# A Macaron layer with a selective scan on one core: the softplus correction in the other half of delta's tile, two buffers for normalised tiles, sixteen weight blocks

## The chip, the cores and the metric

The kernel runs on one core of a Trainium2 chip. The metric is device time in microseconds (us) from launch to end, the median of several runs. A core has a matrix engine (TensorE, PE, with a separate path for weight loads, PEld), a vector engine (DVE), a scalar engine (ACT), GpSimd (POOL) and SyncE (SP), whose queue issues nearly all transfers of this kernel. Each engine works through its own queue in order, and they meet at semaphores.

## The reference

The input is x of shape (4, 1024, 512): four sequences of 1024 tokens, 512 wide, all in float32. Three residual blocks follow each other:

```python
x = x + 0.5 * ffn(layernorm(x))       # gated FFN, 512 -> 1408 -> 512
x = x + mamba(layernorm(x))           # selective scan, inner width 1024, 16 states
x = x + 0.5 * ffn(layernorm(x))       # the same FFN weights again
# ffn:   g = (x @ gate_w.T) * gate_s; u = (x @ up_w.T) * up_s
#        out = ((silu(g) * u) @ down_w.T) * down_s
# mamba: h, gate = split(x @ W_in.T); h = silu(causal_conv4(h) + conv_b)
#        ts, Bm, Cm = split(h @ Wx.T), each rms-normalised
#        delta = softplus(ts @ Wdt.T + dt_bias)
#        s = exp(delta * A) * s + delta * Bm * h      # over time, per channel and state
#        y = (sum over states of s * Cm) + D * h; out = (y * silu(gate)) @ Wout.T
```

## The kernel before

The tokens are cut into 16 chunks (`NCS`) of 256 tokens (`T`), four to a sequence. Chunk k is one stage of the main loop. In stage k the scan of chunk k runs beside "background" work: the gate products of chunk k, the projection back (`tail`) of chunk k - 1, the input projection, convolution and parameters of chunk k + 1, and an FFN over three or four tiles of 128 tokens. `BESIDE[k]` says how many of these tiles belong to the first FFN and how many to the second. An opening (`front`) does the FFN of the first four tiles, and an ending (`back_end`) that of the last four.

The scan of a stage is 32 units: eight channel blocks `i` times four state groups `g`. A unit takes exponentials on ACT (L573), forms delta * u * B on POOL (L578, tile `sb`), scans on DVE (L582), multiplies by C on DVE (L592), and a later fold sums over states on PE (L604, tile `yps`). Before that, delta and delta * u of a channel block must lie on the scan's partition layout: `rows` writes a tile `dd` to DRAM and `spread` reads it back four times as `rep`.

`head(k, i)` makes `dd` for two channel blocks at a time, in eight small steps called chores, one of which is done in each unit. With t = dt + bias, softplus is computed as max(t, 0) + log(1 + exp(-|t|)). ACT writes |t| to `z` and max(t, 0) to `de`, the first half of `dd` (L498, L499), then exp and log (L502, L503). POOL makes the rounding error of 1 + z: e = (1 + z) - 1 (L521), e - z (L506), and takes it from the log (L507). Then POOL completes `de` (L510) and writes delta * u into the second half of `dd` (L511). `dd` has two buffers; `z`, `e` and `lg` have one each.

Normalisation: `stats` takes mean and variance on DVE, POOL makes the factors (`roots`, L214 to L216), and ACT writes the normalised tile `xn` (L218). `flip` transposes it with four PE instructions (L235), and ACT copies the result out (L238). The steps are deferred by one background piece each; `flips` begins tile n + 2 when it has flipped tile n. `xn` comes from a pool with three buffers.

Weights: blocks of 128 x 512 floats stream from DRAM for every chunk through a ring of `RING` = 14 tiles, with the tag `w`. `queue` lists all pieces of work that use blocks, in the order in which they are emitted. After each piece, `do` gives its blocks back and calls `fetch`, which emits loads, in that order, until `LEAD` = 12 blocks are held:

```python
while queue and sum(map(len, held.values())) < LEAD:
    ...
    t = ring.tile([P, H], F32, tag="w", name=f"w_{name}")
```

A piece of `gate`, `up` or W_in holds one block until it is emitted. The eleven blocks of `down_w` and the eight of `Wout` are held until the last part of their stage of work; the projection back is emitted in four parts (two token tiles, each in two halves). When a block of `down_w` comes in for the first time, in the opening, DVE scales it (L133) and it is stored back to DRAM. All loads, stores, rows and spreads are issued by SP in the order in which they are emitted (`load`, L101). Stores of x1 and x2 are emitted two pieces after their sum (`write(2)`).

Of the kernel before, what the change touches and what calls it, by code (L numbers as in the profile page):

```python
# [8 lines left out]
F32 = mybir.dt.float32  # L9
# [4 lines left out]
P = 128  # L14
B, L, H = 4, 1024, 512
# [7 lines left out]
T = 256  # L23
# [8 lines left out]
HEAD = 11  # L32
BEHIND = 1
HALVES = 14
LEAD = 12
FRONT = 5
RING = 14

BESIDE = [(3, 0), (3, 0), (2, 2), (2, 2), (1, 2), (2, 2), (2, 2), (2, 1), (2, 2), (2, 2), (2, 1), (2, 2), (2, 2), (1, 2), (0, 3), (0, 3)]

# [2 lines left out]
def macaron_kernel(ctx: ExitStack, tc: tile.TileContext, a: dict, out: bass.AP):  # L43
# [2 lines left out]
    small = ctx.enter_context(tc.tile_pool(name="small", bufs=4))  # L46
    p1 = ctx.enter_context(tc.tile_pool(name="p1", bufs=1))
    p2 = ctx.enter_context(tc.tile_pool(name="p2", bufs=2))
    p3 = ctx.enter_context(tc.tile_pool(name="p3", bufs=3))
    p4 = ctx.enter_context(tc.tile_pool(name="p4", bufs=4))  # L50
    px = ctx.enter_context(tc.tile_pool(name="px", bufs=HALVES))
    p8 = ctx.enter_context(tc.tile_pool(name="p8", bufs=8))
    ring = ctx.enter_context(tc.tile_pool(name="ring", bufs=RING))
    dram = ctx.enter_context(tc.tile_pool(name="scratch", bufs=1, space=bass.MemoryType.DRAM))
# [65 lines left out]
    def fetch():  # L120

        while queue and sum(map(len, held.values())) < LEAD:
            w = queue[0]
# [30 lines left out]
    def defer(parts, emit):  # L154

        deferred.append([parts, emit])
# [45 lines left out]
    def stats(src, name):  # L202

        stt = small.tile([P, nc.vector.BN_STATS_DIM], F32, tag="st", name=f"st{name}")
        mv = small.tile([P, nc.vector.BN_AGGR_DIM], F32, tag="mv", name=f"mv{name}")
        ve = small.tile([P, 1], F32, tag="ve", name=f"ve{name}")
        rs = small.tile([P, 1], F32, tag="rs", name=f"rs{name}")
        nb = small.tile([P, 1], F32, tag="nb", name=f"nb{name}")
        nc.vector.bn_stats(stt, src)
        nc.vector.bn_aggr(mv, stt)  # L210
        xn = p3.tile([P, H], F32, tag="xn", name=f"xn{name}")

        def roots():
            pin(nc.gpsimd.tensor_scalar(ve, mv[:, 1:2], EPS, None, ALU.add))  # L214
            pin(nc.gpsimd.tensor_tensor(rs, ve, neg_half[:, 0:1], ALU.pow))
            pin(nc.gpsimd.tensor_scalar(nb, mv[:, 0:1], rs, -1.0, ALU.mult, ALU.mult))  # L216

        left = [roots, lambda: pin(nc.scalar.activation(xn, src, AF.Identity, bias=nb, scale=rs))]  # L218

        def more():  # L220
            if left:
                left.pop(0)()
                defer(1, more)

        defer(1, more)
        return xn, left
# [16 lines left out]
    class FFN:  # L243
# [17 lines left out]
        def stats(self, t):  # L261
            return stats(self.x[t], f"f{self.name}_{t}")
# [84 lines left out]
    def prep_stats(k, j):  # L347
        return stats(st[k]["xi", j], f"m{k}_{j}")
# [128 lines left out]
    def head(k, i):  # L477

        d = st[k]
        nm = f"{k}_{i}"  # L480
        dp = ps_m.tile([P, 2, T], F32, tag="mm", name=f"dp{nm}")
        z = p1.tile([P, 2, T], F32, tag="z", name=f"z{nm}")
        e = p1.tile([P, 2, T], F32, tag="e", name=f"e{nm}")
        lg = p1.tile([P, 2, T], F32, tag="lg", name=f"lg{nm}")
        dd = p2.tile([P, 2, 2, T], F32, tag="dd", name=f"dd{nm}")
        de = dd[:, :, 0, :]

        def products():
            for q in range(2):
                nc.tensor.matmul(  # L490
                    dp[:, q, :], lhsT=w_dt[:, (i + q) * P : (i + q + 1) * P], rhs=d["tsT"],
                    start=True, stop=True,
                )

        def split():
            for q in range(2):
                b = dt_b[:, i + q : i + q + 1]
                pin(nc.scalar.activation(z[:, q, :], dp[:, q, :], AF.Abs, bias=b))  # L498
                pin(nc.scalar.activation(dd[:, q, 0, :], dp[:, q, :], AF.Relu, bias=b))  # L499

        def logs():
            pin(nc.scalar.activation(z, z, AF.Exp, scale=-1.0))  # L502
            pin(nc.scalar.activation(lg, z, AF.Ln, bias=1.0))  # L503

        def correct():
            pin(nc.gpsimd.tensor_tensor(e, e, z, ALU.subtract))  # L506
            pin(nc.gpsimd.tensor_tensor(lg, lg, e, ALU.subtract))  # L507

        def complete():
            pin(nc.gpsimd.tensor_tensor(de, de, lg, ALU.add))  # L510
            pin(nc.gpsimd.tensor_tensor(dd[:, :, 1, :], de, d["u"][:, i : i + 2, :], ALU.mult))  # L511
            d["dd", i] = dd[:, 0]
            d["dd", i + 1] = dd[:, 1]

        return [
            products,
            split,
            logs,
            lambda: None,
            lambda: None,  # L520
            lambda: pin(nc.gpsimd.tensor_scalar(e, z, 1.0, 1.0, ALU.add, ALU.subtract)),  # L521
            correct,
            complete,
        ]
# [251 lines left out]
    settle()  # L776
    between = gate_0[FRONT:]
    chores = head(0, 0)
    while chores:
        chores.pop(0)()  # L780
# [3 lines left out]
    for w in between[:2]:  # L784
        do(w)
    chores = head(0, 2)
    while chores:
        chores.pop(0)()
# [6 lines left out]
    for k in range(NCS):  # L795
# [18 lines left out]
        for i in range(NI):  # L814
            for g in range(NS):
                unit(k, i, g)
                if i == 0 and k:
                    gated(k - 1, NI - NS + g)
                if len(summed) >= NS + BEHIND:
                    for _ in range(NS):  # L820
                        add_up()
                n += 1
                done, vector = done + unit_t, vector + unit_v
                while parts and (
                    done * total_v < vector * total
                    or (length - len(parts)) * (units - HEAD) < upto * min(n, units - HEAD)
                ):
                    c, v = step()
                    done, vector = done + c, vector + v
                k2, i2 = ahead(2)  # L830
                if i % 2 == 0 and g == 2 and k2 < NCS:
                    assert not chores
                    rows(k2, i2)
                    rows(k2, i2 + 1)
                k2, i2 = ahead(3)
                if i % 2 == 1 and g == 1 and k2 < NCS:
                    while more and i2 == 0 and ready[k] in parts:
                        c, v = step()
                        done, vector = done + c, vector + v
                    chores += head(k2, i2)  # L840
                    chores.pop(0)()
# [77 lines left out]
```

## Time and profile before

| what | value |
|---|---|
| median of 3 runs | 3204.71 us (3203.93 to 3205.31) |
| the profiled execution: its own time / its span | 3208.17 us / 3206.3 us |
| granted TensorE clock, mean over the span | 0.986 |
| transfers | 506.43 MB, mean 158 GB/s |
| weight loads W_in, gate_w, up_w (256 KB each), median from issue to landing | 3.6, 4.0, 4.1 us |
| L578 POOL scan product, 128x512 | 1275 ns, 1024 times |
| L582 DVE scan with a state, 128x256 | 740 ns, 1536 times |
| L218 ACT normalised tile of the FFN, 128x512 | 814 ns, 56 times |

The span runs from the first to the last instruction; the execution's own time has what lies around it as well. "Busy" is the time in which an engine had an instruction of the program in work. A row of waits reads: who waited, for whom, us in total, how often, the longest. For SP, whose instructions are all the sequencer's, a wait is counted from its instruction before. A row of a group reads: line, engine, operation, out<-in, shapes, count, then busy us and mean ns of one, then the engine's idle time before it and who ended that. "L521" is line 521 of the kernel's file. PE matmul counts are of the chip's instructions, two for each float32 matmul of the program.

### The profile page before, as it was taken

The page shows a single profiled execution, that of the slowest core. Times are in us where ns is not written, and L with a number is a line of the kernel's source. Part 1 is how long each engine was busy: PE and PEld are TensorE (multiplying, and loading weights), DVE is VectorE, ACT ScalarE, POOL GpSimd, SP SyncE. Part 2 cuts the span into 40 slices and gives each one's busy share as a digit, 9 for nine tenths or more (in the row PEclk, how much of TensorE's full clock was granted, in tenths as well). Part 3 has the DMA queues.
Part 4 walks back from the last instruction along what each step waited for, and adds up shares of the span by engine and source line. Part 5 has one row for each costly group of instructions (what it writes and reads, how often), then busy time and mean ns, then how long its engine had stood idle before and what let it go on. Part 6 is the DMA issues. An engine that isn't in the chain of part 4 may idle for free.

```text
span 3206.3 us, 41927 instructions
## 1 busy us (share of the span) xinstructions
PE 3059.7 (95%) x12448; PEld 1644.7 (51%) x12448; DVE 2477.8 (77%) x4981; ACT 1780.1 (56%) x3531; POOL 1938.5 (60%) x1895
## 2 busy tenths in 40 slices
PE   8988899999999999999999999999999999899999
PEld 3554454545555454545545454554555455454434
DVE  1259788888869887887988788798878779798931
ACT  3265555747465664646565474656557475656530
POOL 0066758566766766666675756667575667658610
PEclk9999999999999999999999999999999999999999
DMA  5364566556566655645665654656565564566531
GB/s 171 113 174 119 158 188 171 161 137 184 134 174 181 178 161 148 184 123 160 191 178 159 164 164 123 183 165 171 168 178 161 140 186 132 170 183 178 169 94 43
DMA packets 287427, 506.43 MB, mean 158 GB/s; under 512 B 32097, under 2 KB 50273, under 8 KB 287201
## 3 DMA queue, kind: packets, MB, share of 16 engines
q1 hardware_dynamic: 285616, 503.31, 55.8%
q8 instruction: 100, 1.64, 0.2%
q14 instruction: 127, 1.03, 0.1%
q10 hardware_dynamic: 1584, 0.45, 0.1%
HBM read 442.03 MB, written 61.60 MB: 157 GB/s over the span
## 4 chain that ended last, share of the span: by engine, by line
PE 63%; DVE 21%; ACT 6%; POOL 5%; issue 5%; DMA 1%; DVEq 0%; SPq 0%; POOLq 0%; ACTq 0%
DVE da L582 12%; PE fo L319 12%; PE gate_w L273 12%; PE up_w L273 9%; PE hp L376 5%; PE op L637 5%; PE gp L545 5%; PE yps L604 5%; DVE sb L592 4%; POOL sb L578 3%; ACT da L573 2%; PE gate_wp L273 1%; PE gate_we L273 1%; PE dp L490 1%; PE foe L319 1%
## 5 line engine op out<-in xcount | busy, mean ns | idle before, releaser
L578 POOL TENSOR_TENSOR sb<-rep,bc 128x512 f32<-128x512 f32 x1024 | 1279.4, 1275 | 421.3 <-PE yps L604 302.8
L582 DVE TENSOR_TENSOR_SCAN da<-da,state,sb 128x256 f32<-128x256 f32 x1536 | 1059.7, 740 | 250.9 <-ACT da L573 215.6
L573 ACT ACTIVATE da<-rep,a_w 128x256 f32<-128x256 f32 x2048 | 899.5, 472 | 508.9 <-DVE sb L592 488.0
L592 DVE TENSOR_TENSOR sb<-da,bc 128x512 f32<-128x512 f32 x1024 | 688.8, 680 | 1.7 <-issue 0.4
L273 PE MATMUL gate_w<-fxT,w_gate_w 128*128 128x384 f32 (+1 forms) x1408 | 564.2, 547 | 8.6 <-ACT hd L287 6.3
L273 PE MATMUL up_w<-fxT,w_up_w 128*128 128x384 f32 (+1 forms) x1408 | 557.8, 546 | 3.0 <-DVE hd L304 2.4
L319 PE MATMUL fo<-w_down_w,hd 128*128 128x512 f32 x1232 | 549.4, 599 | 0.0
L273 PEld LDWEIGHTS gate_w<-fxT,w_gate_w 128*128 128x128 f32 x1408 | 268.1, 193 | 256.2 <-issue 154.9
L604 PE MATMUL yps<-sb,fold 128*32 128x256 f32 x4096 | 332.0, 389 | 62.8 <-DVE sb L592 54.1
L273 PEld LDWEIGHTS up_w<-fxT,w_up_w 128*128 128x128 f32 x1408 | 260.7, 190 | 254.1 <-issue 150.8
L582 DVE TENSOR_TENSOR_SCAN da<-da,sb 128x256 f32<-128x256 f32 x512 | 322.6, 679 | 78.6 <-ACT da L573 62.2
L319 PEld LDWEIGHTS fo<-w_down_w,hd 128*128 128x128 f32 x1232 | 230.1, 192 | 273.0 <-issue 271.5
L521 POOL TENSOR_SCALAR e<-z 128x512 f32<-128x512 f32 x64 | 124.4, 1944 | 237.3 <-ACT z L502 223.1
L604 PEld LDWEIGHTS yps<-sb,fold 128*32 128x32 f32 x4096 | 127.7, 110 | 271.4 <-DVE sb L592 122.9
L376 PE MATMUL hp<-mxT,w_W_in 128*128 128x259 f32 x1024 | 244.3, 386 | 23.1 <-issue 12.4
L545 PE MATMUL gp<-mxT,w_W_in 128*128 128x256 f32 x1024 | 244.7, 388 | 4.0 <-ACT dd L499 3.3
L376 PEld LDWEIGHTS hp<-mxT,w_W_in 128*128 128x128 f32 x1024 | 192.5, 191 | 83.5 <-issue 30.4
L637 PE MATMUL op<-w_Wout,u 128*128 128x512 f32 x512 | 228.1, 595 | 0.3 <-POOL u L616 0.3
L545 PEld LDWEIGHTS gp<-mxT,w_W_in 128*128 128x128 f32 x1024 | 195.4, 193 | 63.0 <-issue 19.8
L387 DVE SCALAR_TENSOR_TENSOR u<-hp,conv_w,u 128x256 f32<-128x256 f32 x384 | 178.0, 473 | 14.7 <-ACT u L380 12.2
L287 ACT ACTIVATE hd<-gate_w,gate_s 128x384 f32<-128x384 f32 (+1 forms) x176 | 110.5, 629 | 130.4 <-PE gate_w L273 129.6
L304 DVE SCALAR_TENSOR_TENSOR hd<-up_w,up_s,hd 128x384 f32<-128x384 f32 (+1 forms) x176 | 118.2, 672 | 69.0 <-PE up_w L273 68.9
(112 smaller groups left out, 2649.9 us busy)
## 6 DMA issues: line engine op xcount, KB each, us to landing
rep<-row SPq DMA_DIRECT2D x512, 256.0 KB, 4.9
w_W_in<-in_W_in_dram SPq DMA_DIRECT2D x256, 256.0 KB, 3.6
w_gate_w<-in_gate_w_dram SPq DMA_DIRECT2D x198, 256.0 KB, 4.0
w_up_w<-in_up_w_dram SPq DMA_DIRECT2D x198, 256.0 KB, 4.1
w_down_w<-down_w SPq DMA_DIRECT2D x187, 256.0 KB, 2.7
row<-dd SPq DMA_DIRECT2D x128, 256.0 KB, 3.4
w_Wout<-in_Wout_dram SPq DMA_DIRECT2D x128, 256.0 KB, 4.6
bc<-bcd SPq DMA_DIRECT2D x64, 256.0 KB, 4.9
```

What stands on the lines that cost most here:

```text
L273: nc.tensor.matmul(o[:, : self.n], lhsT=w[:, k, :], rhs=self.xT[:, k, : self.n], start=(k == 0), stop=(k == KH - 1),)
L319: nc.tensor.matmul(op, lhsT=self.hd[:, it, t * P : (t + 1) * P], rhs=wd[it], start=(it == 0), stop=(it == NF - 1),)
L376: nc.tensor.matmul(hp[:, : K - 1 + T], lhsT=w[:, kk, :], rhs=st[k]["xnT"][:, kk, :], start=(kk == 0), stop=(kk == KH - 1),)
L387: pin(nc.vector.scalar_tensor_tensor(u[:, i, :], hp[:, q : q + T], conv_w[:, i, q : q + 1], u[:, i, :], ALU.mult, ALU.add,))
L521: lambda: pin(nc.gpsimd.tensor_scalar(e, z, 1.0, 1.0, ALU.add, ALU.subtract)),
L545: nc.tensor.matmul(gp[:, :T], lhsT=w[:, kk, :], rhs=st[k]["xnT"][:, kk, K - 1 :], start=(kk == 0), stop=(kk == KH - 1),)
L573: e = nc.scalar.activation(da[:, j, :], rep[:, h + j, 0, :], AF.Exp, scale=a_w[:, b0 + h + j, g : g + 1])
L578: nc.gpsimd.tensor_tensor(sb, rep[:, hs, 1, :], d["bc"][:, g : g + 1, :].to_broadcast([P, 2, T]), ALU.mult)
L582: nc.vector.tensor_tensor_scan(da[:, j, :], da[:, j, :], sb[:, j, :], 0.0 if first else state[:, b0 + h + j, g : g + 1], ALU.mult, ALU.add,)
L592: nc.vector.tensor_tensor(sb, da, d["bc"][:, NS + g : NS + g + 1, :].to_broadcast([P, 2, T]), ALU.mult)
L604: nc.tensor.matmul(yp[j * Q : (j + 1) * Q, :], lhsT=fold, rhs=pr[j // 2][:, j % 2, :], start=(g == 0), stop=(g == NS - 1),)
L637: nc.tensor.matmul(op, lhsT=st[k]["u"][:, i, j * P : (j + 1) * P], rhs=wo[i], start=(i == 0), stop=(i == NI - 1),)
```

## The change

Three edits. The ring has 16 blocks for 14, and 14 may be held for 12. The normalised tile `xn` comes from the pool with two buffers, and the pool with three is gone. The tile `e` is gone: `e` now names the second half of `dd`, in which the correction stays until L511 overwrites it with delta * u. Each freed buffer has 2 KB per partition (512 floats), as has each new block of the ring. The four parts of the projection back, the order of the work and all sums are as before.

```diff
-LEAD = 12
+LEAD = 14
 FRONT = 5
-RING = 14
+RING = 16
...
-    p3 = ctx.enter_context(tc.tile_pool(name="p3", bufs=3))
...
-        xn = p3.tile([P, H], F32, tag="xn", name=f"xn{name}")
+        xn = p2.tile([P, H], F32, tag="xn", name=f"xn{name}")
...
         z = p1.tile([P, 2, T], F32, tag="z", name=f"z{nm}")
-        e = p1.tile([P, 2, T], F32, tag="e", name=f"e{nm}")
         lg = p1.tile([P, 2, T], F32, tag="lg", name=f"lg{nm}")
         dd = p2.tile([P, 2, 2, T], F32, tag="dd", name=f"dd{nm}")
-        de = dd[:, :, 0, :]
+        de, e = dd[:, :, 0, :], dd[:, :, 1, :]
```

## Prediction

> **What bounds the kernel now.** I read the page's busy times and chain first, to know which engine can move the end.
>
> ```profile
> PE 3059.7 (95%) x12448; PEld 1644.7 (51%) x12448; DVE 2477.8 (77%) x4981; ACT 1780.1 (56%) x3531; POOL 1938.5 (60%) x1895
> PE 63%; DVE 21%; ACT 6%; POOL 5%; issue 5%; DMA 1%; DVEq 0%; SPq 0%; POOLq 0%; ACTq 0%
> ```
>
> TensorE (PE) is busy all but 146.6 us of the span of 3206.3 us, and the matmuls are not touched by the change. So whatever is gained must come out of those 146.6 us. An average hides where they lie, so I next cut the span into its sixteen stages (a stage begins with its first scan) and asked for the busy times of two: stage 2, with four FFN tiles, and stage 4, with three. The columns are stretch, length, then busy time of PE, PEld, DVE, ACT, POOL.
>
> ```profile
> 532.60:723.90 191.30, 188.96 (x764) 99.23 (x761) 156.56 (x326) 107.91 (x216) 120.04 (x118) 0.99 0.57 159
> 910.10:1081.60 171.50, 160.60 (x730) 92.57 (x728) 146.68 (x325) 109.08 (x223) 123.03 (x121) 1.00 0.62 176
> ```
>
> Stage 2 has 2.3 us of PE idle: nothing to win, and 35 us of idle DVE as cover. Stage 4 has 10.9. The same cut over all stages gives 2.3 to 3.6 us in each of the eight four-tile stages, 9.3 to 13.3 in the seven three-tile ones after stage 0, 27.9 in stage 0, and 9.5 ahead of the first transpose. Third, I asked what PE waits for, because the ring of weight blocks can only pay where PE waits for weights.
>
> ```profile
> PE yps L604 <- DVE sb L592: 54.1, 47, 3.9
> PE dp L490 <- DVE tsT L455: 22.4, 15, 2.1
> PE hp L376 <- issue: 12.4, 11, 5.9
> ```
>
> No row of PE or PEld names a weight transfer, except that the 12.4 us in front of the convolution products have no cause named. I paired each of the 652 loads of W_in, gate_w and up_w with the first of its eight matmuls, in order: the least time from landing to use is 7.1 us (the very first block), then 8.1; the median is 26.9. The unnamed 5.9 us are not a late weight.
>
> Fourth, SyncE's (SP's) queue, since every load passes through it.
>
> ```profile
> SPq L101 <- PE up_w L273: 420.8, 134, 6.2
> SPq L101 <- DVE xo L645: 247.3, 28, 20.9
> ```
>
> ```profile
> 948.15 0.38 SPq L101 DMA_DIRECT2D w_gate_w<-in_gate_w_dram  x1
> 968.60 0.33 SPq L101 DMA_DIRECT2D x<-xo  x1
> 969.01 0.88 SPq L101 DMA_DIRECT2D w_W_in<-in_W_in_dram  x2
> ...
> 976.80 0.89 SPq L101 DMA_DIRECT2D row<-dd  x2
> ...
> 981.64 1.75 SPq L101 DMA_DIRECT2D rep<-row  x4
> ```
>
> ```profile
> 990.04 1.27 POOL L578 TENSOR_TENSOR sb<-rep,bc 128x512 f32<-128x512 f32 x1 [11.57 <-DMA rep<-row]
> ```
>
> SP stands 20 us at a store of x2 whose sum (L645) is not made, then issues a burst of weight loads, and only then the row and the spread that GpSimd (POOL) needs: POOL idles 11.57 us. Such stalls of 11.6 to 12.3 us stand in stages 4, 7, 10, 13 and 14, and one of 8.9 in stage 0. This is the sensitive spot.
>
> **The change part by part.** *Ring 14 to 16, LEAD 12 to 14.* When r blocks have been given back, the newest load is number r + LEAD, and its slot was last held by number r + LEAD - RING. That is r - 2 before (12 - 14) and r - 2 after (14 - 16). So at every place in SP's queue stands a load, as now, that waits for the same matmuls as now; only which block it brings is two later. The 420.8 us are waits that stay. The burst after the store is as long as now, because one give-back of Wout's eight blocks frees eight loads under either LEAD; the stores, rows and spreads are passed by none of it. Two more loads stand at the start, ahead of ffn[0]'s tiles: 2 x 0.47 us of issue and 2 x 0.65 us of transfer (the spacing of issues and landings in the burst), about 1.3 us for tiles that L218 first normalises at 124.2 us. Gain: weights land two blocks sooner, but nothing on PE waits for them: 0. If the unnamed 12.4 us were weights after all, that would be the gain; I take 0, by the margin of 7.1 us. In the opening, the eleven scalings of down_w (L133) move two blocks ahead on DVE, their store with them; DVE is busy 11.0 of the 40 us from 40 to 80, so they are covered. Uncovered, eleven times the 2 us waits for their landings would be 22 us; they feed a store that is read in stage 0 only, so I take 0.
>
> *The correction e inside dd.* POOL's writes at L521 and L506, and the read at L507, go to two rows of 256 with 1 KB between, instead of 512 in one piece.
>
> ```profile
> L521 POOL TENSOR_SCALAR e<-z 128x512 f32<-128x512 f32 x64 | 124.4, 1944 | 237.3 <-ACT z L502 223.1
> L506 POOL TENSOR_TENSOR e<-e,z 128x512 f32<-128x512 f32 x64 | 81.7, 1276 | 1.5
> ...
> L510 POOL TENSOR_TENSOR dd<-dd,lg 128x512 f32<-128x512 f32 x64 | 81.5, 1273 | 1.6 <-POOL back L362 0.2
> ```
>
> L510 already works on the split half and takes 1273 ns; L506 works in one piece and takes 1276. So 0.2 us over 64 calls for L506 and as much for L507. L521 is another operation, not shown split: between 0 and a doubling, 64 x 1.94 = 124 us of POOL; a gain is excluded, since no element is saved. I take 0, as L510 is near in everything but the operation. POOL holds 5% of the chain with 60% busy, so one us in twelve shows: 0 to 10 us, kept for the range. [...] A new wait: L521 now writes into dd, whose slot must be free of the row transfers two heads back; the Relu (L499) into the same dd waits for those already, and L521 comes after L499 through z. Zero; were that cover gone, POOL's scan products behind L521 would wait for a row, 3.4 us from issue to landing.
>
> *xn in two buffers.* L218 on ACT must now wait for the transposes of two tiles back, not three. Pairing the 96 writes with the 384 transposes in order, 90 of the 94 that have a tile two back come 0.5 us or more after its transposes ended (median 53). Four come before, by 1.05 to 1.18 us; one, in ACT's and PE's timelines:
>
> ```profile
> 687.17 0.80 ACT L218 ACTIVATE xnf<-xf,nbf,rsf 128x512 f32<-128x512 f32 x1
> 688.26 0.59 ACT L238 COPY fxT<-tpf 128x512 f32<-128x512 f32 x1 [0.29 <-PE tpf L235]
> ```
>
> ```profile
> 687.57 0.65 PE L235 MATMUL tpf<-ident,xnf 128*128 128x128 f32 x4
> ```
>
> There ACT gets 4 x 1.1 = 4.4 us of new wait, all in four-tile stages. Behind it stand the copy-out L238 and the exponentials of the scan; DVE, which wants them, has 33 us idle in such a stage, and the tile itself is transposed only at 709.3. Taken as 0; if the cover were gone, 4.4 us.
>
> The sum is 0 on the profiled execution's 3208.17 us. That stands 3.5 us over the median of 3204.71, so I forecast the median, 3205.
>
> [...]
>
> **The rivals.** *Same time, 66%.* A measurement of this kernel cannot tell less than about 0.2%, 6.4 us. Not every instruction runs in written order (the L218 above runs ahead of an earlier copy-out), so other slots may shuffle neighbours; but the four three-tile stages with one or two tiles of each kind last 171.5 to 174.4 us, so seven stages moved at random by some 1.5 us make about 4 us.
>
> *Faster, 14%.* The spread after the store comes sooner. If two loads of each burst went out ahead of the stall, row and spread would come 1.3 us sooner in six stages: 8 us, 3197. If the five stalls vanished, those stages' PE idle (10.9, 12.0, 10.6, 9.3, 13.3) would fall to 2.4 each: 44 us, 3161. I put this case at 3192, near the smaller. Against it stands the count of loads, which is equal.
>
> *Slower, 20%.* One mechanism: ACT, in order, is held at L218 for PE, with the exponentials behind it. If the write is placed as early as the slot lets it, ACT waits as long as the copy-outs do (ACT fxT on PE tpf: 110.6 us in 21 waits, longest 9.3). ACT has 6% of the chain with 56% busy, so one us in nine shows: 12 us, 3217. It decides from 58 us of such waits on. With a doubled L521 on top, 10 us more: 3227.
>
> *No effect as said* (the slots stay unused) is the same time again.
>
> **The numbers.** 3205; the likeliest case alone spans 3198 to 3212. The range of 3188 to 3230 takes in the smaller end of the faster case and both slower mechanisms; it leaves out the vanished stalls.
>
> **What would show it.** Right: SP's wait for up_w near 420; POOL's waits for rep in the same stages, 79 us in all, within 15; W_in's least margin after the stall from 8 to about 12 us; L521 at 1.94 us; a few waits of L218 for tpf of about 1 us; PE busy within 5 us of 3059.7. Wrong: four-tile stages with over 5 us of PE idle; the rep stalls shorter or gone; L521 over 3 us; L218 waiting for tpf by tens of us.

## The result and the profile after

The changed kernel takes 3223.26 us (median of 4 runs, 3222.87 to 3224.99) against 3204.32 us of the kernel before in the same set: ratio 1.0059, 95% interval 1.0046 to 1.0072. It is 18.9 us slower. The profiled execution took 3222.87 us, its span 3220.9 us; the span before was 3206.3 us. The time lies inside the range of the prediction, but the likeliest case, no change, was not what happened.

The edit shifts line numbers a little (L521 is now L519, L578 is L576, L210 is L209, L214 is L213). The page of the changed kernel, its busy times and its chain:

```profile
PE 3063.1 (95%) x12448; PEld 1641.6 (51%) x12448; DVE 2479.7 (77%) x4981; ACT 1780.9 (55%) x3534; POOL 1936.2 (60%) x1895
PE 68%; DVE 16%; POOL 6%; ACT 5%; issue 4%; DMA 1%; SPq 0%; DVEq 0%; POOLq 0%; ACTq 0%
```

PE is busy 3.4 us longer with the same instructions, and idle 11 us longer. ACT has three instructions more, which the change did not ask for: loads of its function tables (1.28 us each), all three in stage 15. Next the same cut into stages, first the two that the prediction showed (2 and 4), then 1, 13 and 14:

```profile
529.17:719.74 190.57, 188.25 (x764) 98.97 (x761) 156.32 (x326) 107.73 (x215) 120.06 (x118) 0.99 0.57 159
905.96:1075.71 169.75, 158.41 (x730) 92.51 (x728) 147.21 (x325) 108.73 (x223) 122.96 (x121) 0.99 0.63 178
347.50:529.17 181.67, 159.84 (x714) 90.89 (x710) 153.92 (x325) 107.48 (x220) 119.00 (x117) 0.94 0.58 164
2557.40:2742.76 185.36, 172.47 (x743) 96.83 (x741) 153.75 (x323) 107.61 (x220) 125.01 (x121) 0.96 0.58 166
2742.76:2929.06 186.30, 167.37 (x734) 94.45 (x733) 153.09 (x323) 106.94 (x218) 119.76 (x116) 0.95 0.56 160
```

Stages 1, 13 and 14 of the kernel before, for comparison:

```profile
352.40:532.60 180.20, 167.55 (x732) 95.68 (x730) 154.20 (x326) 108.59 (x220) 119.90 (x118) 0.95 0.58 166
2563.73:2737.73 174.00, 164.69 (x730) 94.06 (x728) 152.96 (x322) 107.99 (x220) 121.68 (x117) 0.99 0.60 171
2737.73:2916.28 178.55, 165.25 (x732) 93.68 (x730) 152.96 (x324) 107.58 (x218) 119.96 (x116) 0.99 0.59 167
```

Stages 2 and 4 are as short as before. Up to stage 13 the changed kernel is even ahead: stage 13 begins 6.3 us sooner (2557.4 for 2563.7), most of it won in stage 0 (151.9 us for 156.0). Then stage 13 is 11.3 us longer, stage 14 7.8 us, stage 15 1.9 us. The granted clock in the two long stages is 0.96 and 0.95 for 0.99. So nothing general has become slower: stages 13 and 14 have, and a third place is hidden by a cut at the first scan. PE begins stage 1's gate products (`gp`) 12.7 us ahead of the kernel before and stage 2's only 4.1 us ahead, and in stage 1 it idles 21.8 us for 12.6.

The waits of PE in the changed kernel, and those of SP:

```profile
PE yps L602 <- DVE sb L590: 45.7, 40, 3.9
PE dp L488 <- DVE tsT L454: 37.6, 15, 7.3
PE gate_w L272 <- ACT hd L286: 14.2, 7, 5.1
```

```profile
SPq L100 <- PE up_w L272: 411.5, 134, 5.1
SPq L100 <- DVE xo L643: 243.7, 25, 20.9
```

SP waits as before, so the deeper ring changed little in its queue. But dp now waits up to 7.3 us for tsT (2.1 before), and the gate products up to 5.1 us for ACT. Three timelines say why.

First POOL in stage 13, where it stands still in front of a one-column instruction of an FFN tile's normalisation (L213), with the scan products (L576) behind it:

```profile
2681.72 2.50 POOL L576 TENSOR_TENSOR sb<-rep,bc 128x512 f32<-128x512 f32 x2
2695.98 0.22 POOL L213 TENSOR_SCALAR vef<-mvf 128x1 f32<-128x1 f32 x1 [11.75 <-DVE mvf L209]
```

DVE did the aggregate (L209) that POOL wants at 2695.72, behind 96 of the stage's 128 scans, although the statistics that it reads (L208) had been ready since 2677.6. In the kernel before it stands behind 65 scans.

Second ACT in stage 1 (stage 14 has the same at 2780):

```profile
379.96 0.64 ACT L500 ACTIVATE z<-z 128x512 f32<-128x512 f32 x1
380.62 1.28 ACT L198 ACT_TABLE_LOAD   x1
381.92 1.91 ACT L198 ACTIVATE g<-g 128x2048 f32<-128x2048 f32 x1
383.85 1.28 ACT L501 ACT_TABLE_LOAD   x1
385.14 0.63 ACT L501 ACTIVATE lg<-z 128x512 f32<-128x512 f32 x1
385.79 1.28 ACT L199 ACT_TABLE_LOAD   x1
```

The silu of the gate (L198) has fallen between the softplus's exponential (L500) and its logarithm (L501), and the functions' tables are loaded three times for two. (The kernel before has a load too many in these two stages as well, at another place: both kernels have 11 loads in each.)

Third DVE and PE in stage 1 (stage 14 again alike, 7.31 us at 2871):

```profile
479.40 0.76 DVE L580 TENSOR_TENSOR_SCAN da<-da,state,sb 128x256 f32<-128x256 f32 x1 [4.17 <-POOL sb L576]
480.60 0.76 DVE L580 TENSOR_TENSOR_SCAN da<-da,state,sb 128x256 f32<-128x256 f32 x1 [0.44 <-POOL sb L576]
481.26 0.59 DVE L303 SCALAR_TENSOR_TENSOR hd<-up_w,up_s,hd 128x384 f32<-128x384 f32 x1
481.77 0.41 DVE L454 COPY tsT<-t 128x256 f32<-128x256 f32 x1
```

```profile
482.24 2.07 PE L488 MATMUL dp<-tsT,w_dt 128*128 128x256 f32 x4 [6.96 <-DVE tsT L454]
```

Two scans that must wait for POOL stand ahead of the copy tsT, whose input PE had finished at 475.3.

All three are the same kind of thing: in the queue of an engine that works in order, something stands ahead of an instruction that is wanted sooner. **Theory O** is therefore: the change costs time because the instructions come out in another order, not through memory, transfers or the ring itself. The order of the work is as before in the text of the kernel, but an instruction that is not pinned is issued where the builder puts it, and with loads emitted two blocks sooner it has chosen other places (by what rule, no run shows). Read off the two programs, PE's instruction differs at 694 of 6448 places, DVE's at 838 of 4981, ACT's at 394, POOL's at 4; SP's order is as written in both. With the two freeing edits and the old ring (e1) four instructions of ACT move; the rest comes with the ring. Nearly all of it lies in stages 0, 1, 4, 7, 10, 13, 14 and 15.

### The profile page after: what moved, and what is told of

Its sections match the earlier page's. It is cut to its first block, busy times and chain, and to the rows that moved or that the text cites. A ratio compares the mean times of both kernels' runs of the same rounds, so it can differ in the third digit from the quotient of the medians.

```text
span 3220.9 us, 41906 instructions
## 1 busy us (share of the span) xinstructions
PE 3063.1 (95%) x12448; PEld 1641.6 (51%) x12448; DVE 2479.7 (77%) x4981; ACT 1780.9 (55%) x3534; POOL 1936.2 (60%) x1895
## 4 chain that ended last, share of the span: by engine, by line
PE 68%; DVE 16%; POOL 6%; ACT 5%; issue 4%; DMA 1%; SPq 0%; DVEq 0%; POOLq 0%; ACTq 0%
PE gate_w L272 13%; PE fo L318 13%; DVE da L580 9%; PE up_w L272 8%; PE op L635 7%; PE hp L375 6%; PE yps L602 5%; PE gp L543 5%; POOL sb L576 3%; DVE sb L590 3%; ACT da L571 2%; PE dp L488 1%; PE gate_we L272 1%; PE gate_wp L272 1%; PE foe L318 1%
## 5 line engine op out<-in xcount | busy, mean ns | idle before, releaser
L576 POOL TENSOR_TENSOR sb<-rep,bc 128x512 f32<-128x512 f32 x1024 | 1278.1, 1274 | 426.2 <-PE yps L602 359.2
L571 ACT ACTIVATE da<-rep,a_w 128x256 f32<-128x256 f32 x2048 | 896.6, 472 | 488.0 <-DVE sb L590 465.9
L272 PE MATMUL gate_w<-fxT,w_gate_w 128*128 128x384 f32 (+1 forms) x1408 | 571.3, 552 | 16.5 <-ACT hd L286 14.2
L602 PE MATMUL yps<-sb,fold 128*32 128x256 f32 x4096 | 325.0, 388 | 50.7 <-DVE sb L590 45.7
L519 POOL TENSOR_SCALAR dd<-z 128x512 f32<-128x512 f32 x64 | 124.2, 1941 | 244.2 <-ACT z L500 235.2
L303 DVE SCALAR_TENSOR_TENSOR hd<-up_w,up_s,hd 128x384 f32<-128x384 f32 (+1 forms) x176 | 117.9, 670 | 55.8 <-PE up_w L272 55.6
```

The costliest lines, as they stand in the source:

```text
L272: nc.tensor.matmul(o[:, : self.n], lhsT=w[:, k, :], rhs=self.xT[:, k, : self.n], start=(k == 0), stop=(k == KH - 1),)
L571: e = nc.scalar.activation(da[:, j, :], rep[:, h + j, 0, :], AF.Exp, scale=a_w[:, b0 + h + j, g : g + 1])
L576: nc.gpsimd.tensor_tensor(sb, rep[:, hs, 1, :], d["bc"][:, g : g + 1, :].to_broadcast([P, 2, T]), ALU.mult)
L602: nc.tensor.matmul(yp[j * Q : (j + 1) * Q, :], lhsT=fold, rhs=pr[j // 2][:, j % 2, :], start=(g == 0), stop=(g == NS - 1),)
```

## The experiments

Orders were set by tying each engine's instructions in a given sequence, without any new wait (abridged):

```python
for a, b in zip(places, places[1:]):      # places: the sequence wanted on this engine
    tc.add_manual_dep(made[b], made[a].name, NoSync, reason="arranged")
```

"Before's order" and "after's order" below are the sequences of the two kernels. Each ratio is to the kernel before in the same set of runs. The medians of the kernel before in the four sets run from 3204.32 to 3205.75 us, so a difference between runs of different sets, the changed kernel's 3223.26 us among them, holds to about 1.5 us. That the tying itself costs no time is seen in e5, which ties nearly the whole of after's order and takes 3221.76 us.

| run | ring / held | order | median us | ratio (95%) |
|---|---|---|---|---|
| e1 | 14 / 12, both freeing edits | its own | 3205.69 | 0.9996 (0.9987 to 1.0006) |
| e2 | 16 / 14 | before's | 3204.35 | 0.9996 (0.9987 to 1.0006) |
| e3 | 14 / 12 | after's | 3229.28 | 1.0072 (1.0057 to 1.0087) |
| e4 | 16 / 12 | its own | 3234.19 | 1.0087 (1.0072 to 1.0102) |
| e5 | 16 / 14 | after's, silu behind the log | 3221.76 | 1.0051 (1.0039 to 1.0064) |
| e6 | 16 / 14 | after's, DVE of stages 1, 14 before's | 3216.35 | 1.0036 (1.0024 to 1.0049) |
| e7 | 16 / 14 | after's, stage 13 before's | 3213.50 | 1.0024 (1.0013 to 1.0034) |
| e8 | 16 / 14 | after's, with e5 to e7 together | 3207.85 | 1.0009 (1.0000 to 1.0018) |
| e9 | 16 / 14 | after's, one instruction earlier | 3215.62 | 1.0028 (1.0018 to 1.0039) |
| e10 | 16 / 14 | before's, the same one later | 3216.09 | 1.0033 (1.0020 to 1.0045) |
| e11 | 16 / 14 | after's in stages 0 and 2 to 12, before's in 1, 13 to 15 | 3198.63 | 0.9982 (0.9973 to 0.9991) |
| e12 | 16 / 12 | before's | 3205.16 | 0.9999 (0.9991 to 1.0008) |

### The parts of the change: e1, e2, e3

e1 keeps the two edits that free memory and leaves the ring alone:

```diff
-LEAD = 14
+LEAD = 12
-RING = 16
+RING = 14
```

> The two edits that free memory alone (e in the second half of dd, xn in two buffers), with the ring still at 14 blocks and 12 held. In the program only four instructions of ACT (the four late xn writes) stand elsewhere than before. Theory O (the 19 us are a matter of the order in which the engines issue, which the ring's edit shifts): 3204 +- 2 us. Rival E (the waits of L218 or the split write of L521 cost them): 3215 to 3223 us.

Measured: 3205.69 us, no difference from the kernel before. The freeing edits cost nothing that can be measured. (The ring alone was not run: its two blocks take the memory that these edits free.)

e2 is the changed kernel, with every engine but SP in before's order:

> The changed kernel, with PE, ACT, POOL and DVE made to issue in the order of the kernel before; the loads of the 16-block ring stay where the change puts them in SP's queue. Theory O: the 19 us are gone, 3196 to 3206 us, and no exponential or logarithm has a silu between; whether below 3204 tells if the earlier loads gain anything by themselves. Rival R (earlier loads crowd out rows and spreads): 3218 to 3225 us.

Measured: 3204.35 us. The 18.9 us are gone, with 16 blocks, 14 held and all three edits in place. Its waits of PE are those of the kernel before:

```profile
PE yps L602 <- DVE sb L590: 54.2, 46, 3.9
PE dp L488 <- DVE tsT L454: 22.4, 15, 2.1
```

e3 is the reverse, 14 blocks in after's order:

> The ring of 14 with 12 held (and the two edits that free memory), with PE, ACT, POOL and DVE made to issue in the order of the changed kernel. Theory O: 3219 to 3226 us, with three more table loads on ACT than before. Rival R: 3204 +- 3 us.

Measured: 3229.28 us. Its stages 13 and 14 are 185.3 and 186.5 us long, as in the changed kernel. It is 6 us slower still, above the range of theory O. In the profiled executions, which are 9.0 us apart, 6.8 us of that are in the opening (the first scan starts at 202.4 us for 195.6): four times PE waits for DVE, 4.3 us in all, each time for a product (L303) that stands behind a scaling whose block of `down_w` has come late; in the changed kernel it does not wait there. So the order costs the time, with either ring, and in before's order the two additional blocks bring nothing.

### Another ring, another order: e4, e12

e4 keeps the 16 blocks and holds 12:

```diff
-LEAD = 14
+LEAD = 12
```

> Sixteen slots, but only 12 blocks held, so that SP's queue is as before and only the slots are more; the rest as in the change. The engines' order lies between the two (a third or less of the moved instructions on PE). Theory O: anywhere from 3200 to 3215 us, according to whether a silu falls between an exponential and its logarithm; the table loads tell (175 as before: 3204 +- 4). Rival R (earlier loads): 3204 +- 2 us, as no load is earlier.

Measured: 3234.19 us, the slowest of all, and outside both theories: it has 175 table loads, as before, for which theory O had 3204 +- 4. Here the loss lies elsewhere: stages 3, 5, 7, 8 and 10 to 12 are each 2.6 to 4.8 us longer than before, while stage 14 has the length of before (178.4 us). SP's wait for up_w falls to 246.1 us, since the slot that a load takes was now given back two blocks earlier (r + 12 - 16 = r - 4 in the prediction's count).

e12 is the same ring in before's order:

> 16 slots and 12 held, as in the run that took 3234 us, but with every engine but SyncE in the order of the kernel before. Theory O (the 29 us there are again the order): 3203 to 3208, SyncE's wait for up_w still near 246 us. Theory Q (SyncE, which waits less for blocks, brings rows and spreads late or early): over 3220, with dp's waits for tsT of 2.1 to 2.5 us in the four-tile stages as there.

```profile
SPq L100 <- PE up_w L272: 248.7, 84, 5.7
```

Measured: 3205.16 us. SP waits 172 us less for up_w than in the kernel before (248.7 for 420.8), and the time is the same; the 29 us of e4 were the order, too. Which instructions of that order cost them was not traced.

### The three places: e5 to e8

> The changed kernel in its own order, but for two neighbours on ACT in stages 1 and 14: the silu of the gate stands behind the logarithm L501 and not between the exponential L500 and it. Theory O (the order makes local gaps, each worth what it shows): table loads fall from 178 to 176 (one 1.28 us load less in each of the two stages); the PE waits of 5.1 us at 384 and 2780 and the half-clock windows of 10.2 us behind them go, so up to 5.1 + 10.2/2 = 10 us a place; I expect 3209 to 3217. Theory N (what is late next takes it: the late tsT at 475 and 2871 in the same stages sets the end anyway): under 4 us, 3219 to 3224.

On ACT's queue, in stages 1 and 14:

```diff
 L500 exp z
-L198 silu g      (and its table loads)
 L501 log lg
+L198 silu g
```

Measured: 3221.76 us, 1.5 less than the changed kernel, no more than the sets differ by, and the intervals overlap. The two table loads are gone, and PE's wait behind them fell from 5.12 to 3.84 us, by one load of 1.28 us and no more. The rival was right: the disorder that is the most striking in the timeline is worth next to nothing.

> The changed kernel in its own order on PE, ACT and POOL; DVE alone issues stages 1 and 14 in the order of the kernel before, where the tsT copies stand ahead of two scans that wait for POOL. Theory O: PE's waits of 6.96 us (475) and 7.31 us (2871) for tsT fall to 2.1 or less and the half clock behind them goes: some 5 + 4 us a place, 3206 to 3216. Theory N (DVE's order alone moves the wait to the scans' readers, yps or the silu's late z): under 4 us, 3219 to 3224.

Measured: 3216.35 us, 6.9 less than the changed kernel, between the two theories and nearer to O. Stage 1 is 3.3 us shorter and stage 14 4.2 us, and the waits of 7 us for tsT are gone (longest 3.3).

> The changed kernel in its own order, but for stage 13, which every engine issues in the order of the kernel before (with it the aggregate L209 of mvf14_2 stands ahead of the scans of the last units). Theory O: stage 13 falls from 185.4 us to 174 plus or minus 2 and POOL's idle 11.7 us at 2696 goes; the other stages stay, so 3212 plus or minus 2. Theory N (the time saved turns up as a longer wait in stage 14 or 15): stage 13 short, stages 14 and 15 longer by more than half of it, over 3217.

Measured: 3213.50 us, 9.8 less, as theory O had it. Stage 13 itself is 179.5 us, not 174: part of the gain shows elsewhere.

> The three edits of this set together: silu behind the log, DVE's stages 1 and 14 and all of stage 13 in the order of the kernel before; all else as in the changed kernel. Theory O: the three places hold the whole difference and the rest of the order is as good or better (it was 6 to 8 us ahead up to stage 13): 3192 to 3203. Theory N: the gains don't add, over 3210. If it lies under 3199 it is faster than both kernels.

Measured: 3207.85 us, between the theories: 15.4 us come back, where the three alone add up to 18.2. PE begins stage 14's gate products 9.1 us ahead of the kernel before and stage 15's 5.2 us ahead, and the end is 0.8 us behind. What is left sits in stages 14 and 15, where PE and ACT, and in stage 15 DVE, still have after's order.

### One instruction: e9, e10

In stage 13 the whole order of four engines was put back. Is it the one aggregate that POOL waits for?

```diff
 DVE, stage 13:
 L208 statistics of tile 14_2
+L209 aggregate  of tile 14_2
 ...                             36 others: scans, products by C, copies
-L209 aggregate  of tile 14_2
```

It moves 36 places, and in the changed kernel it stands behind 96 of the stage's 128 scans; the two expectations count 37, and call its place the end of the stage's scan work.

> The changed kernel in its own order, but for a single instruction: in stage 13 DVE's aggregate of mvf14_2 (L209) stands right behind its statistics (L208), 37 instructions sooner than in the changed kernel, where it is the last of stage 13's scan work. Theory O1 (that instruction holds POOL's L213, and the scan products behind it, for 11.7 us): POOL's idle at 2696 goes, stage 13 falls from 185.4 us to between 177 and 181 as with the whole stage's order put back (179.5), and the time is 3212 to 3216. Theory O2 (the rest of stage 13's order costs it): stage 13 stays over 184, time 3220 to 3225.

> The reverse: 16 slots and 14 held, every engine in the order of the kernel before (3204.35 us in that form), but for the same single instruction, which in stage 13 is put 79 places later, to the end of stage 13's scan work, where the changed kernel has it. Theory O1: POOL idles 8 to 12 us ahead of L213 in stage 13, the stage grows from 172.4 us by 6 to 11, and the time is 3210 to 3216. Theory O2: under 2 us more.

POOL's L213 in e9, then in e10:

```profile
2683.97 0.22 POOL L213 TENSOR_SCALAR vef<-mvf 128x1 f32<-128x1 f32 x1
```

```profile
2702.51 0.22 POOL L213 TENSOR_SCALAR vef<-mvf 128x1 f32<-128x1 f32 x1 [11.47 <-DVE mvf L209]
```

Measured: e9 3215.62 us, 7.6 less than the changed kernel, with stage 13 at 176.4 us for 185.4. e10 3216.09 us, 11.7 more than the same kernel without the move (e2), with stage 13 at 181.9 us for 172.4. One instruction of 0.17 us, moved and nothing else, is worth 8 us one way and 12 the other. O1 holds in both directions, within 0.6 us of its bounds: in e10 POOL stands for 11.5 us, the stage is 9.5 us longer and the whole 11.7. (The profiled execution of e9, at 3210.9 us the lowest of its seven, flatters the stage by some of the 5 us to the median.)

### The better half of each: e11

> 16 slots and 14 held; stages 1, 13, 14 and 15 in the order of the kernel before, stages 0 and 2 to 12 in the order of the changed kernel. Theory O: it enters stage 13 some 7 to 12 us ahead of the kernel before (the changed kernel is 10 to 12.7 us ahead when stage 1's products begin, and loses 8.6 of it in its own stage 1), and keeps that: 3192 to 3199, faster than both kernels. Theory N (the lead is given back in stages 14 and 15, where the weights or the convolution set the end): over 3202.

Measured: 3198.63 us over 11 runs, ratio 0.9982 (0.9973 to 0.9991): the only one of the kernels that is faster than the kernel before, by 6.6 us or 0.2%. Its runs spread from 3194.31 to 3203.97 us. In the profiled execution (3194.31 us, the lowest of them, against one of the kernel before that stood 3.5 us over its median) it enters stage 13 11.8 us ahead of the kernel before and keeps that. So the new order was not worse throughout. It was better in stage 0 above all (151.7 to 153.6 us in the runs with after's order there, 155.4 to 156.2 with before's), and bad in stages 1, 13, 14 and 15, by which alone e11 differs from the changed kernel: 24.6 us.

## Why the prediction was right and wrong

**The ring: right.** The count of loads (the slot waited for is r - 2 in both) gives an unchanged queue: SP's wait for up_w was 411.5 us in the changed kernel and 420.9 in e2, for 420.8. That PE waits for no weights, so that blocks landing sooner gain nothing, is shown by e2 and e12: in e2 the median time from landing to first use is 32.2 us for 26.9, and the time is the same. The least margin of W_in's blocks rose from 8.1 us to 13.5 in the changed kernel (forecast: about 12). PE's repeating waits for DVE at yps are no shorter with 16 blocks either: in before's order (e2) they last 54.2 us, for 54.1.

**The correction in `dd`: right.** The value taken from L510 held for the other operations as well:

```profile
L519 POOL TENSOR_SCALAR dd<-z 128x512 f32<-128x512 f32 x64 | 124.2, 1941 | 244.2 <-ACT z L500 235.2
L504 POOL TENSOR_TENSOR dd<-dd,z 128x512 f32<-128x512 f32 x64 | 81.4, 1272 | 1.5
```

1941 ns for 1944 and 1272 for 1276: the split rows cost nothing that shows in these times.

**`xn` in two buffers: right in before's order.** The forecast was four waits of 1.1 us. This is ACT's L217 in e2, us and times:

```profile
  PE tpf L234: 4.5, 4
```

In the changed kernel these waits don't appear, because there the four writes stand behind the copy-out. The rival of a held ACT did not come to pass.

**The spread waits: wrong.** They were to stay within 15 of 79 us, and fell to 43.8. e2 has 71.3 and e3, with 14 blocks in after's order, 32.7: that, too, is the order and not the loads. The stalls that I had priced at up to 44 us of gain shrank by 35 us, and no time came of it; in stages 4, 7 and 10 of the changed kernel they last 5.4 us, nothing and 4.7 us for 11.6 to 11.9, and PE idles 11.0 to 11.4 us there (10.6 to 12.0 before). That idle time, which the rival would have given back, was not theirs.

**The step that failed** is the sentence in the rivals that not every instruction runs in written order and that neighbours may be shuffled, "seven stages moved at random by some 1.5 us make about 4 us". The mechanism was named, with L218 as its witness, but it was put down to the slots and mis-sized. It moved stage 13 by 11.3 us, 14 by 7.8, 15 by 1.9 and 1 by 1.4, and stages 0 and 4 by -4.1 and -1.8. The seven stages that I took the size from stood in one order, so their likeness said nothing about another. The bound to take was what one shuffle can do where it hits, an engine's queue held for some ten us, in more than one stage, and not the 1.5 us by which stages of the same order differ. Nor does an average tell what such a hold costs: by the shares of the chain one us in twelve of POOL's was to show, while in e10 a hold of 11.5 us showed 11.7. (The spread stalls, just as long on POOL's row, cost nothing that was seen when they shrank.) The rival on the slower side had the right sign by the wrong mechanism, and that the range took in 3223.26 us is luck: its upper end was made for a held ACT and a doubled L521, neither of which came.

Since the order also gains, its bad places cost more than the 18.9 us: the 24.6 us between the changed kernel and e11. The three places give back 15.4 us together (e8). The 9.2 us between e8 and e11 are left; against the kernel before, e8 loses 3.9 us in stage 14 and 6.0 in stage 15. Which instructions of those it is was not tried. One suspect is the three table loads more of stage 15, 1.28 us each: at 2940.8, 2966.3 and 2983.2 an exponential (L571) has come between a silu and the load that follows it. No run moves them alone. Nor was it traced why the builder placed the aggregate so late.

## What to carry to other kernels

Where a framework chooses the order of instructions, an edit that touches only buffers and prefetch depth can be an edit of the order on several engines, and its price is then that of the late instructions, not of the buffers (here 3223.26 us in the new order and 3204.35 in before's, with the same buffers): compare the two orders before pricing anything else. Pin the small instructions on which another engine's queue hangs (here an aggregate of 0.17 us). And when two orders differ, cut both into stages: the best time may lie in taking each stage from the better one, as in e11.

## What the runs showed of the hardware

Two small gaps on PE came with a halved clock. In stage 13 of the changed kernel PE waits 2.75 us from 2707 and 2.78 us from 2712, and this is what the windows over it show (length, busy times, clock in the third column from the end):

```profile
2700.00:2711.00 11.00, 8.25 (x29) 3.12 (x27) 7.88 (x18) 4.21 (x11) 11.00 (x10) 0.99 0.00 0
2711.00:2721.00 10.00, 7.22 (x22) 2.80 (x21) 9.50 (x19) 4.42 (x11) 10.00 (x9) 0.50 0.27 92
```

Two rows of matmuls of 512 columns, ahead of these gaps and behind them:

```profile
2700.82 6.17 PE L318 MATMUL fo<-w_down_w,hd 128*128 128x512 f32 x14
...
2717.96 2.77 PE L318 MATMUL fo<-w_down_w,hd 128*128 128x512 f32 x3
```

The clock is halved for 10.2 us from 2710.8, and a matmul of 512 columns takes twice as long there: three in 2.77 us (they start 0.85 us apart), for 14 in 6.17 us (0.43 us apart). PE is busy for 7.22 us of the second window, so the half clock cost some 3.6 us there beside the 5.5 us of the two gaps (an estimate, half of the 7.22 us). The first gap ended at 2709.7, 1.0 us before the half clock began; the second lies inside it. A shorter gap was followed by a half clock as well: in the kernel before, one of 1.62 us, which ended at 2031.9, by 3.4 us of it, from 2032.8. But not every gap is: after one of 2.55 us, which ended at 1028.8 in the changed kernel, the granted clock was 1.00 up to 1041. What decides between them, these runs do not show.
